# A graph layer on one core: each row transfer of blocks 9 to 117 waits for TensorE at the same share of the next block's work

## The chip, the core and the metric

The kernel runs on one core of one Trainium2 chip. The core has a matrix engine (TensorE, PE in the profile; its weight loads are shown apart as PEld), three engines for elementwise work (VectorE or DVE, ScalarE or ACT, GpSimd or POOL), a sync engine (SP) that starts transfers, and 16 DMA engines that move data between the chip's memory and the core's on-chip buffers. The metric is the device time of one execution in microseconds (us); lower is better.

## The reference

A graph has 6250 nodes and 206,250 edges. Each edge passes a message through a small two-layer network; the messages are averaged at the node at one end of the edge, and the result goes through a second network, a residual connection and a layer norm. `x` holds 64 features for each node, `edge_attr_64` 64 for each edge.

```python
edge_index = jnp.stack([src, dst])
row, col = (edge_index[0], edge_index[1])
msg = jnp.concatenate([src_node_features[col], edge_attr], axis=1)
h = jax.nn.relu(msg @ W1a.T + b1a)
h = h @ W1b.T + b1b
sums = jax.ops.segment_sum(h, row, num_segments=n_nodes)
counts = jax.ops.segment_sum(jnp.ones((h.shape[0],), h.dtype), row, num_segments=n_nodes)
agg = sums / jnp.maximum(counts, 1.0)[:, None]
z = jnp.concatenate([src_node_features, agg], axis=1)
z = jax.nn.relu(z @ W2a.T + b2a)
z = z @ W2b.T + b2b
out = jnp.concatenate([z, src_node_features], axis=1) @ Wr.T + br
...
x = _layernorm(x + out, axis=-1, eps=1e-05)
```

Everything is float32. The time lies in the part up to `sums`: the first layer of the edges, and the sum over the edges of each node.

## The kernel before

The edges are cut into tiles of 128, and the tiles into 124 blocks of 13 (`NG`, `BLK`; `NGR` is 124). For each block the kernel computes the first layer's output `h` of its 1664 edges (128 features plus two columns, so rows of 130 floats), and GpSimd writes these rows out to a table in the chip's memory, each row at a slot that depends on the edge's node, so that the rows of nearby nodes come to lie together (a bin is 128 nodes). Later, groups of the table are read back (`rt`, line 1454) and summed by node: a matmul with a one-hot matrix (line 1502), in small pieces spread over the following blocks.

**How a tile's rows come about.** In blocks 4 to 103 the first tiles of a block are joined in threes: TensorE multiplies one-hot marks by the loaded data (`join`, line 1264, six matmuls 512 wide, whose result ScalarE copies at line 1269), which lays the 384 edges of three tiles into 128 groups of four places, and then computes their messages (`join_rows`, line 1277, finished by ScalarE at line 1280). The output of a join is written by one transfer, called a quad (line 1363). A block has two joins (six tiles), or three in the odd blocks from 9 to 25 (`THRICE`), or none below 4 and from 104 on. The other tiles of a block are direct: line 1352 multiplies, ScalarE applies the relu into `orow` (line 1355), and each tile is written by a transfer of its own (line 1392), called a row transfer. So GpSimd issues 9 transfers for a block with two joins, 7 with three, 13 with none. `orow` is a ring of four blocks (`ROWS`).

**One iteration** of the loop handles block k. On TensorE it holds, in this order: the counts for block k+1 (lines 1091 to 1130), a first part of the direct tiles, a first part of a group of sums (`sum_first`), the last direct tiles, the joins, the rows of the joins, and the rest of the sums (`sum_rest`). Where sums are due faster, more of them follow.

**What sets the order.** The order of TensorE, ScalarE, VectorE and SP is written out by hand. GpSimd's queue is not: a scheduler lays out the transfers by the time at which it expects their inputs, and an instruction waits in the queue behind those ahead of it. `scatter(k)` emits the transfers of block k, and it runs two iterations behind (`LEAD`). In blocks 9 to 117 (`PACED`) some row transfers also wait for a named instruction of TensorE in iteration k+1, taken from the dictionary `done`: the last matmul of a direct tile (`done[k, c]`), of a join's rows (`"join0"` and so on), of the first half of the sums (`"first"`), or of their rest (`"rest"`). With two joins (`j0` is 6) four of the seven row transfers have such a wait; with three joins three of the four, since the block behind has only two joins; with none four of thirteen, since the block behind has no join. The others, and the quads, wait only for their own data and the queue.

## Time and profile before

| | before |
|---|---|
| median of 3 runs | 2108.51 us (2105.86 to 2118.02) |
| the profiled execution, its own time | 2113.43 us |
| span of the profiled execution | 2111.6 us |
| mean granted TensorE clock | 0.874 |
| TensorE busy, matmuls | 1648.5 us, 78% |
| VectorE busy | 1376.4 us, 65% |
| GpSimd busy | 1153.6 us, 55% |
| ScalarE busy | 1105.0 us, 52% |

The page of the profile gives busy times, an overview of the span in 40 slices, the chain of work that ended last, and the costliest groups of instructions, with what ended the idle time ahead of them. A timeline lists single instructions with their start, their duration and the idle time of their engine before them. A table of windows gives, for stretches of the span, the busy time of each engine and in brackets the number of its instructions, then the granted TensorE clock (1.00 is full), the mean busy share of the DMA engines, and GB/s. "Issue" is time in which an engine waited for nothing that the profile shows; "remote" and "another core or an unknown queue" are releases that the profile can't place. There is one core here, so these aren't other cores.

In the profiled execution, blocks 9 to 26 run from about 185 to 360 us, blocks 27 to 103 from there to about 1528, and the blocks without joins from there to about 2050, of which the last six, 118 to 123, are not in `PACED`.

### The profile page before, as it was taken

To read this page: it belongs to the slowest core of one execution; us is meant where nothing else is said; L and a number is where in the kernel's file an instruction comes from. 1 tells how busy PE (TensorE), PEld (TensorE's weight loads), DVE (VectorE), ACT (ScalarE), POOL (GpSimd) and SP (SyncE) were. 2 spreads that over 40 slices of the span, in tenths; PEclk is the share of its full clock that TensorE was granted. 3 is DMA by queue.
4 is the path that set the end of the run, shared out by engine and by line. 5 is a ranking of instruction groups with operands and counts; after the bars stand their busy time and mean duration, and the time that the engine had idled before them with its cause. 6 is when DMAs were issued, how large, how long until landed. Compare 5 with 4: busy or idle time off the path is not lost.

```text
span 2111.6 us, 33441 instructions
## 1 busy us (share of the span) xinstructions
PE 1648.5 (78%) x10901; PEld 1455.0 (69%) x10901; DVE 1376.4 (65%) x3210; ACT 1105.0 (52%) x2246; POOL 1153.6 (55%) x1268
## 2 busy tenths in 40 slices
PE   5577877768887888788778887877867778677787
PEld 4466766657776777677667776776767667566676
DVE  5377777656667777677776777776755555454377
ACT  2257777666666566566666666656622223222007
POOL 6464655565555566566665665655655545544400
PEclk7578988889999899999998999989978878777899
DMA  6556667665656567566556555555668667565472
GB/s 163 162 171 220 234 224 243 214 211 176 209 183 204 169 201 211 169 195 188 181 174 182 175 173 163 186 157 170 168 201 277 200 190 208 170 183 172 147 216 66
DMA packets 243142, 396.32 MB, mean 188 GB/s; under 512 B 43621, under 2 KB 177895, under 8 KB 242703
## 3 DMA queue, kind: packets, MB, share of 16 engines
q1 hardware_dynamic: 162109, 225.24, 37.7%
q0 software_dynamic: 48240, 121.28, 16.4%
q10 hardware_dynamic: 32610, 47.58, 6.5%
q8 instruction: 89, 1.46, 0.3%
q14 instruction: 94, 0.77, 0.1%
HBM read 218.49 MB, written 175.44 MB: 187 GB/s over the span
## 4 chain that ended last, share of the span: by engine, by line
PE 57%; issue 11%; DVE 10%; ACT 10%; another core or an unknown queue 8%; DMA 3%; POOL 1%; SPq 0%; ACTq 0%; DVEq 0%; POOLq 0%
PE h_ps L1502 22%; PE h_ps L1264 10%; PE h_ps L1352 9%; PE h_ps L1277 7%; DVE oh L1483 2%; DVE marks L1232 2%; ACT rhs L1317 2%; ACT rj L1269 1%; ACT orow L1355 1%; DMA rows<-orow,rowidx 1%; DMA rt<-rows 1%; ACT orow L1280 1%; ACT marks L1237 1%; PE cnt_ps L1091 1%
## 5 line engine op out<-in xcount | busy, mean ns | idle before, releaser
L1392 POOL DMA_INDIRECT rows<-orow,rowidx x985 | 947.2, 962 | 769.4 <-issue 207.4
L1502 PE MATMUL h_ps<-rt,oh 128*128 128x129 f32 x4056 | 602.3, 303 | 126.4 <-issue 105.4
L1502 PEld LDWEIGHTS h_ps<-rt,oh 128*128 128x128 f32 x4056 | 554.3, 215 | 151.9 <-issue 135.7
L1355 ACT ACTIVATE orow<-h_ps 128x384 f32<-128x384 f32 (+1 forms) x287 | 153.3, 537 | 657.5 <-PE h_ps L1352 360.7
L1277 PE MATMUL h_ps<-mv,rj 128*128 128x130 f32 x1672 | 256.1, 305 | 136.3 <-ACT rj L1269 73.5
L1264 PE MATMUL h_ps<-marks,side 128*128 128x512 f32 x1254 | 343.7, 423 | 23.8 <-ACT xr_now L1652 10.6
L1277 PEld LDWEIGHTS h_ps<-mv,rj 128*128 128x128 f32 x1672 | 232.6, 210 | 174.4 <-ACT rj L1269 89.1
L1562 DVE TENSOR_TENSOR part<-part,h_ps 128x387 f32<-128x387 f32 (+2 forms) x249 | 122.6, 493 | 312.5 <-remote 147.7
L1483 DVE TENSOR_TENSOR oh<-ramp,rt 128x768 f32<-128x768 bf16 (+3 forms) x440 | 321.3, 765 | 7.2 <-DMA rt<-rows 7.0
L1352 PE MATMUL h_ps<-mv,rhs 124*128 124x128 f32 x1970 | 297.3, 298 | 16.8 <-issue 9.2
L1264 PEld LDWEIGHTS h_ps<-marks,side 128*128 128x128 f32 x1254 | 245.1, 204 | 79.5 <-issue 11.6
L1352 PEld LDWEIGHTS h_ps<-mv,rhs 124*128 124x128 f32 x1970 | 267.1, 209 | 20.4 <-issue 10.6
L1232 DVE TENSOR_TENSOR marks<-quad_ramp,ramp 128x1024 fp32r<-128x1024 f32 x209 | 250.9, 1204 | 0.0
L1363 POOL DMA_INDIRECT quads<-orow,qidx x209 | 200.4, 959 | 88.8 <-ACT orow L1280 39.1
L1280 ACT ACTIVATE orow<-h_ps 128x260 f32<-128x260 f32 x418 | 142.6, 388 | 90.8 <-PE h_ps L1277 28.0
L1105 DVE TENSOR_SCALAR of_quads<-cnt_ps 128x98 bf16<-128x98 f32 x100 | 26.6, 266 | 247.0 <-remote 84.2
L1269 ACT COPY rj<-h_ps 128x512 f32<-128x512 f32 x209 | 118.8, 588 | 120.8 <-PE h_ps L1264 67.6
L1238 ACT ACTIVATE marks<-marks,ones 128x512 fp32r<-128x512 f32 x209 | 151.0, 722 | 6.8
L1237 ACT ACTIVATE marks<-quad_ramp,z_act 128x512 fp32r<-128x512 f32 x209 | 149.5, 715 | 0.0
L1049 DVE TENSOR_TENSOR_SCAN had<-ramp,bins 128x400 bf16<-128x400 bf16 (+1 forms) x124 | 135.0, 1089 | 14.9 <-ACT bins L1070 1.2
L1315 ACT ACTIVATE rhs<-rhs,from_win 60x896 f32<-60x896 bf16 (+1 forms) x116 | 130.4, 1124 | 2.8
L1317 ACT ACTIVATE rhs<-rhs,ones 60x896 f32<-60x896 f32 (+1 forms) x116 | 130.2, 1123 | 2.9
(189 smaller groups left out, 1535.6 us busy)
## 6 DMA issues: line engine op xcount, KB each, us to landing
rt<-rows SPq DMA_DIRECT2D x138, 390.0 KB
rt<-quads SPq DMA_DIRECT2D x98, 390.0 KB
rhs<-in_edgeT SPq DMA_DIRECT2D x91, 224.0 KB
rt<-rows SPq DMA_DIRECT2D x103, 195.0 KB
enat<-in_edgeJ SPq DMA_DIRECT2D x91, 192.0 KB
rows<-orow,rowidx POOLq DMA_INDIRECT x985
rows<-padrow ACTq DMA_DIRECT2D x12, 1300.0 KB
quads<-padrow ACTq DMA_DIRECT2D x11, 1300.0 KB
```

The lines of the kernel that those rows point to most:

```text
L1232: nc.vector.tensor_tensor(m[:, :n, :], all_q[:, None, :].to_broadcast([P, n, QUAD * P]), z[:, :n, None].to_broadcast([P, n, QUAD * P]), op ...
L1237: nc.scalar.activation(m[:, t, :], all_q, AF.Square, bias=z_acts[k][:, i * JOIN + t : i * JOIN + t + 1], scale=-1.0)
L1264: nc.tensor.matmul(ps, s[:, p, i * JOIN + t, :], m[:, t, :], start=t + p == 0, stop=t == JOIN - 1 and p == 1,)
L1277: done[k, f"join{i}"] = nc.tensor.matmul(ps[:, j, :], rj[:, (g0 + j) * P : (g0 + j + 1) * P], m, start=True, stop=True).ins.name
L1280: nc.scalar.activation(mrow[:, g0 : g0 + 2, :], ps, AF.Relu)
L1317: nc.scalar.activation(rhs[D:WIDE, :], rhs[D:WIDE, :], AF.Relu, bias=ones[D:WIDE, :1], scale=-1.0)
L1352: done[k, c] = nc.tensor.matmul(ps[:, j, :], rhs[:WIDE, of * P : (of + 1) * P], m[:WIDE, :H], start=True, stop=True).ins.name
L1355: nc.scalar.activation(orow_of(k, k0, n)[:, :, :H], ps[:, :n, :], AF.Relu)
L1363: s = nc.gpsimd.indirect_dma_start(out=qep.rows.rearrange("(q r) f -> q (r f)", r=QUAD), out_offset=bass.IndirectOffsetOnAxis(ap=qidx[:, q ...
L1392: s = nc.gpsimd.indirect_dma_start(out=ep_.rows, out_offset=bass.IndirectOffsetOnAxis(ap=rowidx[:, k % RING * BLK + j : k % RING * BLK + j ...
L1483: nc.vector.tensor_tensor(res[:, at_tile : at_tile + nb * n, :], ramp[:, None, :].to_broadcast([P, nb * n, P]), node[:, :, None].to_broadc ...
L1502: m = nc.tensor.matmul(of_bin(b), oh[:, at_tile, :], rt[:, j * n + t, : H + 1], start=t0 + t == st.lo[b], stop=t0 + t == st.hi[b] - 1,)
```

## The change

The dictionary `pace` goes, and with it `done`. Every piece of TensorE's work in an iteration now notes its size and its last matmul in `phases`: a group of direct tiles counts 4·H for each tile, a join 2·3·4·128, a pair of a join's rows 8·W, a piece of sums 4·(H+1) for each of its tiles. Every row transfer of blocks 9 to 117 then waits for the last piece of block k+1 whose cumulated work is not above a share of the whole. The share rises evenly with the tile's number, and the quads, which have no such wait, count as the first transfers.

```diff
+        phases = [[] for _ in range(NGR + 1)]
+        def phase(k, work, name):
+            phases[k].append(((phases[k][-1][0] if phases[k] else 0) + work, name))
+        def reached(k, share):
+            names = [name for at, name in phases[k] if at <= share * phases[k][-1][0]]
+            return names[-1] if names else phases[k - 1][-1][1]
...
-            pace = (
-                {9: BLK - 1, 10: "join0", 11: "join1", 12: "join2"} if j0 == 3 * JOIN
-                else {6: 9, 8: BLK - 1, 10: "join0", 12: "join1"} if j0 == 2 * JOIN
-                else {j0: 9, j0 + 2: "first", 7: BLK - 1, 9: "join0", 11: "rest"}
-            )
...
-                later = (min(k + 1, NGR - 1), pace.get(j))
-                if k in PACED and later in done:
+                later = reached(k + 1, (j - j0 + joined(k)) / (BLK - j0 + joined(k))) if k in PACED else None
+                if later:
                     tc.add_manual_dep(
-                        s.ins, done[later],
+                        s.ins, later,
                         mybir.DependencyInfo(mybir.DependencyClass.Sync, mybir.DependencyReason.DATA),
```

The order of TensorE, ScalarE, VectorE and SP is the same in both programs, and so are TensorE's waits. GpSimd's order and waits differ from the first paced blocks on.

The first place is GpSimd's queue around block 41, in the stage with two joins. `orow_141` to `orow_144` are the ring's buffers, here for blocks 40, 41, 42 and 43; `rows_64` is the table of the direct tiles' rows, `quads` that of the joins. `DMASW` is one of the queue's own eight counters, `PE_49`, `DVE_49` and `Activation_49` are waits for TensorE, VectorE and ScalarE. Before, in iteration 41:

```order
L1392 DMA rows_64<-orow_141,rowidx 125440x130 [waits DMASW3_49,PE_49]
L1392 DMA rows_64<-orow_142,rowidx 125440x130 [waits DMASW4_49,DVE_49,Activation_49]
L1392 DMA rows_64<-orow_142,rowidx 125440x130 [waits DMASW5_49]
L1392 DMA rows_64<-orow_141,rowidx 125440x130 [waits DMASW6_49,PE_49]
L1392 DMA rows_64<-orow_142,rowidx 125440x130 [waits DMASW7_49,Activation_49]
L1392 DMA rows_64<-orow_141,rowidx 125440x130 [waits DMASW0_49,PE_49]
L1363 DMA quads<-orow_142,qidx 54976x520 [waits DMASW1_49,DVE_49,Activation_49]
L1392 DMA rows_64<-orow_141,rowidx 125440x130 [waits DMASW2_49,PE_49]
L1363 DMA quads<-orow_142,qidx 54976x520 [waits DMASW3_49,Activation_49]
```

And now, from the first row transfer of block 41, which waits for iteration 42:

```order
L1401 DMA rows_64<-orow_142,rowidx 125440x130 [waits DMASW1_49,PE_49]
L1401 DMA rows_64<-orow_142,rowidx 125440x130 [waits DMASW2_49,PE_49]
L1401 DMA rows_64<-orow_142,rowidx 125440x130 [waits DMASW3_49,PE_49]
L1401 DMA rows_64<-orow_142,rowidx 125440x130 [waits DMASW4_49,PE_49]
L1401 DMA rows_64<-orow_142,rowidx 125440x130 [waits DMASW5_49]
L1401 DMA rows_64<-orow_142,rowidx 125440x130 [waits DMASW6_49,PE_49]
L1401 DMA rows_64<-orow_142,rowidx 125440x130 [waits DMASW7_49,PE_49]
L1377 DMA quads<-orow_143,qidx 54976x520 [waits DMASW0_49,DVE_49,Activation_49]
L1377 DMA quads<-orow_143,qidx 54976x520 [waits DMASW1_49,Activation_49]
```

Before, three rows of the block's own iteration stood between four of the block before it. Now all seven rows of a block stand together, each behind TensorE's work on the next block, and the two quads of that next block follow them. In iteration 42, which has 85 matmuls in the trace, the waits of before fall behind matmuls 13, 39, 59 and 67, and those of now behind 33, 39, 45, 51, 59 and 67, the rows without a wait of their own behind the one ahead of them.

The second place is the same queue in the stage without joins, around block 110, whose rows are in `orow_143` (`orow_142` is block 109). Before, in iteration 110:

```order
L1392 DMA rows_64<-orow_143,rowidx 125440x130 [waits DMASW4_49,DVE_49,Activation_49]
L1392 DMA rows_64<-orow_143,rowidx 125440x130 [waits DMASW5_49]
L1392 DMA rows_64<-orow_142,rowidx 125440x130 [waits DMASW6_49,PE_49]
L1392 DMA rows_64<-orow_143,rowidx 125440x130 [waits DMASW7_49,Activation_49]
L1392 DMA rows_64<-orow_143,rowidx 125440x130 [waits DMASW0_49]
L1392 DMA rows_64<-orow_143,rowidx 125440x130 [waits DMASW1_49]
L1392 DMA rows_64<-orow_142,rowidx 125440x130 [waits DMASW2_49,PE_49]
L1392 DMA rows_64<-orow_143,rowidx 125440x130 [waits DMASW3_49,Activation_49]
L1392 DMA rows_64<-orow_143,rowidx 125440x130 [waits DMASW4_49]
L1392 DMA rows_64<-orow_143,rowidx 125440x130 [waits DMASW5_49,Activation_49]
L1392 DMA rows_64<-orow_143,rowidx 125440x130 [waits DMASW6_49]
L1392 DMA rows_64<-orow_142,rowidx 125440x130 [waits DMASW7_49,PE_49]
```

And now, the rows of block 110 from the first on:

```order
L1401 DMA rows_64<-orow_143,rowidx 125440x130 [waits DVE_49,DMASW0_49,PE_49,Activation_49]
L1401 DMA rows_64<-orow_143,rowidx 125440x130 [waits DMASW1_49,PE_49]
L1401 DMA rows_64<-orow_143,rowidx 125440x130 [waits DMASW2_49,PE_49]
L1401 DMA rows_64<-orow_143,rowidx 125440x130 [waits DMASW3_49,PE_49]
L1401 DMA rows_64<-orow_143,rowidx 125440x130 [waits DMASW4_49,PE_49,Activation_49]
L1401 DMA rows_64<-orow_143,rowidx 125440x130 [waits DMASW5_49,PE_49]
L1401 DMA rows_64<-orow_143,rowidx 125440x130 [waits DMASW6_49]
L1401 DMA rows_64<-orow_143,rowidx 125440x130 [waits DMASW7_49,PE_49,Activation_49]
L1401 DMA rows_64<-orow_143,rowidx 125440x130 [waits DMASW0_49]
L1401 DMA rows_64<-orow_143,rowidx 125440x130 [waits DMASW1_49,PE_49]
L1401 DMA rows_64<-orow_143,rowidx 125440x130 [waits DMASW2_49,Activation_49]
L1401 DMA rows_64<-orow_143,rowidx 125440x130 [waits DMASW3_49,PE_49]
```

Here the change goes the other way: nine of these twelve rows had no wait for TensorE, and now three have none. In iteration 110, which has about 120 matmuls in the trace, the waits of before fall behind matmuls 24, 42, 80 and 120, and those of now behind 12, 18, 24, 36, 42, 56, 68, 80, 92, 106 and 120.

More of the change, by code (lines that the diff above doesn't have):

```diff
@@ L1263, in join @@
                 for p in range(2):
-                    nc.tensor.matmul(
+                    name = nc.tensor.matmul(
                         ps, s[:, p, i * JOIN + t, :], m[:, t, :],
                         start=t + p == 0, stop=t == JOIN - 1 and p == 1,
-                    )
+                    ).ins.name
+            phase(k, 2 * JOIN * QUAD * P, name)
             rj = turned[k, i] = top.rjs[(join_at[k] + i) % 2]
@@ L1276, in join_rows @@
                 for j in range(2):
-                    done[k, f"join{i}"] = nc.tensor.matmul(
+                    name = nc.tensor.matmul(
                         ps[:, j, :], rj[:, (g0 + j) * P : (g0 + j + 1) * P], m, start=True, stop=True
                     ).ins.name
+                phase(k, 4 * W * 2, name)
                 nc.scalar.activation(mrow[:, g0 : g0 + 2, :], ps, AF.Relu)
@@ L1333, in fast_path @@
         made = {}
-        done = {}
+        phases = [[] for _ in range(NGR + 1)]
[4 more added lines that the diff above has]
+            return names[-1] if names else phases[k - 1][-1][1]
         def low_bits(k):
@@ L1351, in hidden @@
                     of = c - (BLK - direct(k))
-                    done[k, c] = nc.tensor.matmul(
+                    name = nc.tensor.matmul(
                         ps[:, j, :], rhs[:WIDE, of * P : (of + 1) * P], m[:WIDE, :H], start=True, stop=True
                     ).ins.name
+                phase(k, 4 * H * n, name)
                 nc.scalar.activation(orow_of(k, k0, n)[:, :, :H], ps[:, :n, :], AF.Relu)
@@ L1492, in summed @@
         def summed(st, reads, oh, of_bin, bins=None):
-            at_tile = 0
+            at_tile, work = 0, 0
             for b0, nb, t0, n, rt in reads:
@@ L1506, in summed @@
                         at_tile += 1
-            return m.ins.name
+                        work += 4 * (H + 1)
+            return work, m.ins.name
         def reads_of(st):
@@ L1570, in sum_first @@
             g.half = range(g.b0, g.b0 + -(-g.nb // 2))
-            done[k, "first"] = summed(g.st, g.reads, g.oh, lambda b: g.ps[:, b - g.b0, :], g.half)
+            phase(k, *summed(g.st, g.reads, g.oh, lambda b: g.ps[:, b - g.b0, :], g.half))
             return g
@@ L1575, in sum_rest @@
             if g.nb > len(g.half):
-                done[k, "rest"] = summed(
+                phase(k, *summed(
                     g.st, g.reads, g.oh, lambda b: g.ps[:, b - g.b0, :], range(g.half.stop, g.b0 + g.nb)
-                )
+                ))
             totals.append(g)
```

1 line of the change is left out of this document (removed).

## The prediction

> **What bounds the kernel now.** I read the chain of waits first, for no engine is busy all the time.
>
> ```profile
> PE 57%; issue 11%; DVE 10%; ACT 10%; another core or an unknown queue 8%; DMA 3%; POOL 1%; SPq 0%; ACTq 0%; DVEq 0%; POOLq 0%
> ```
>
> TensorE's own work is 57% of the chain, and 19% is time for which the profile names no cause; on a span of 2111.6 us that is some 400 us. GpSimd, the engine whose queue the change rewrites, is 1%. So the second look goes to GpSimd's groups, the page's row and then what waits for it:
>
> ```profile
> L1392 POOL DMA_INDIRECT rows<-orow,rowidx x985 | 947.2, 962 | 769.4 <-issue 207.4
> ...
> L1483 DVE TENSOR_TENSOR oh<-ramp,rt 128x768 f32<-128x768 bf16 (+3 forms) x440 | 321.3, 765 | 7.2 <-DMA rt<-rows 7.0
> ```
> ```profile
> L1392 POOLq EVENT_SEMAPHORE  x720: 17/17/14378, 12.5 to 2001.5; - x180
> ...
> who waited for it (us, times):
>   POOL rows L1392: 0.9, 3
> ```
>
> A transfer holds GpSimd for 0.96 us, and no other engine waits for one; the sums, which read the rows back, lost 7 us to that in all. The transfers would seem free. That they aren't shows where they come in long unbroken runs. Here are five windows in the stage without joins; behind the span come TensorE's matmuls (the first bracket), its weight loads, VectorE, ScalarE, GpSimd, the clock.
>
> ```profile
> 1857.30:1863.30 6.00, 6.00 (x53) 5.78 (x52) 5.83 (x12) 2.63 (x4) 4.28 (x5) 0.97 0.91 234
> 1863.30:1869.70 6.40, 4.19 (x29) 3.28 (x27) 1.73 (x3) 2.07 (x3) 4.33 (x5) 1.00 0.53 159
> 1869.70:1875.80 6.10, 3.67 (x12) 2.89 (x13) 2.16 (x3) 1.17 (x3) 4.79 (x5) 0.63 0.36 92
> 1875.80:1881.80 6.00, 2.69 (x8) 1.75 (x7) 0.00 (x0) 0.00 (x0) 2.88 (x3) 0.50 0.21 73
> 1881.80:1887.80 6.00, 6.00 (x40) 6.00 (x41) 5.04 (x8) 0.00 (x0) 0.00 (x0) 0.74 0.81 271
> ```
> ```profile
> 1857.29 0.96 POOL L1392 DMA_INDIRECT rows<-orow,rowidx  x1 [7.07 <-PE h_ps L1502]
> 1858.55 0.95 POOL L1392 DMA_INDIRECT rows<-orow,rowidx  x1 [0.30 <-PE cnt_ps L1092]
> ...
> 1868.48 0.96 POOL L1392 DMA_INDIRECT rows<-orow,rowidx  x1 [0.90 <-remote]
> ...
> 1878.58 0.96 POOL L1392 DMA_INDIRECT rows<-orow,rowidx  x1 [0.30 <-issue]
> 1888.65 0.95 POOL L1392 DMA_INDIRECT rows<-orow,rowidx  x1 [9.11 <-PE h_ps L1502]
> ```
>
> A run of seventeen transfers starts at 1857.3, one each 1.26 us (1858.55 − 1857.29), with no pause longer than the 0.90 us at 1868.48. For its first 6 us TensorE does 53 matmuls, 8.8 each us; then the rate falls, to 12 in 6.1 us (2.0 each us), and it stays there until the run ends at 1878.6. Two to three microseconds later TensorE is back. The run isn't a result of TensorE's slowness, for GpSimd hardly waits in it. The same at another place, with six transfers in the first window and seven in the second:
>
> ```profile
> 1649.00:1655.50 6.50, 6.50 (x61) 6.50 (x60) 4.64 (x10) 4.86 (x6) 4.12 (x6) 1.00 0.95 278
> 1655.50:1663.90 8.40, 3.74 (x23) 3.31 (x21) 1.16 (x2) 1.01 (x3) 6.55 (x7) 0.75 0.50 140
> ```
>
> So a run may be some five transfers long; what goes beyond that costs TensorE. I call this starving; why it happens the profile doesn't show, only that the 19% without a cause are partly this. Where the runs are short, nothing of the kind is seen. This is GpSimd in the stage with two joins, block 41:
>
> ```profile
> 633.01 0.96 POOL L1392 DMA_INDIRECT rows<-orow,rowidx  x1 [1.16 <-PE cnt_ps L1095]
> 634.27 0.96 POOL L1363 DMA_INDIRECT quads<-orow,qidx  x1 [0.30 <-ACT bins L1070]
> ...
> 638.06 0.96 POOL L1392 DMA_INDIRECT rows<-orow,rowidx  x1 [0.30 <-issue]
> 640.64 0.96 POOL L1392 DMA_INDIRECT rows<-orow,rowidx  x1 [1.62 <-remote]
> 641.90 0.96 POOL L1392 DMA_INDIRECT rows<-orow,rowidx  x1 [0.30 <-issue]
> 647.29 0.96 POOL L1392 DMA_INDIRECT rows<-orow,rowidx  x1 [4.43 <-PE h_ps L1277]
> ```
>
> The named waits break the nine transfers of an iteration into groups, with pauses between starts of 2.6 us (640.64 − 638.06) and 5.4 us. The stages, and an iteration without any disturbance (two rows of the chain that each begin one):
>
> ```profile
> 185.00:360.00 175.00, 138.43 (x872) 118.12 (x871) 124.43 (x333) 135.70 (x279) 103.17 (x107) 0.88 0.70 234
> 360.00:1528.00 1168.00, 953.72 (x6487) 837.75 (x6487) 832.59 (x2015) 750.50 (x1485) 694.97 (x724) 0.92 0.60 185
> 1528.00:1845.00 317.00, 233.66 (x1577) 217.98 (x1575) 160.98 (x271) 81.56 (x113) 169.41 (x178) 0.81 0.68 207
> ```
> ```profile
> 928.54 0.17 PE cnt_ps L1091
> ...
> 939.92 0.17 PE cnt_ps L1091
> ```
>
> In the stage with two joins 724 transfers at nine a block are 80 iterations of 14.5 us (1168/80.4); undisturbed, one takes 11.4 us (939.92 − 928.54). So 3.1 us of each are lost to something, part of it already starving. The stage without joins has 178 transfers, thirteen a block: 13.7 iterations of 23.1 us.
>
> **The change, part by part.** *Two joins (77 blocks, 27 to 103).* Nine transfers, as before, but the three rows that went ahead in the block's own iteration are held, and all seven rows follow each other behind marks that lie 6 to 8 matmuls apart (33 to 67 of 85). At 8.8 matmuls a microsecond a mark is passed each 0.7 to 0.9 us, faster than GpSimd's 1.26. So once the first is passed the others don't hold the queue back, and the two quads behind them, which need the joins, are ready as the rows end. The nine become one run: eight steps of 1.26 are 10.1 us. TensorE is good for the first 6.0, starved until about 2.4 us after the last start (between 1878.58 and 1881.8), so for 6.5 us at 2.0 instead of 8.8 matmuls: 6.5 · (1 − 2.0/8.8) = 5.0 us lost. On 11.4 that is 16.4, against 14.5 now: +1.9 us, 77 times, **+146**. The bounds: if TensorE, once slow, reaches the last marks late, so that two of the nine fall off the run, seven are left; starved from 6.0 to 7.6 + 2.4, 4.0 · 0.77 = 3.1 us, the iteration is 14.5 and the cost nothing. If only half of the 3.1 us lost now is starving and the rest stays, 11.4 + 1.5 + 5.0 = 17.9, +3.4 each and +262. I take +146, which lies between the two. Behind a held row wait the quads, and behind them nothing but later rows; who waits for those was shown above: nobody.
>
> *Three joins (18 blocks, 9 to 26, of which nine have three).* Seven or nine transfers, the runs in part broken by the shorter blocks. Half of the price above, 18 · 0.95 = +17, between 0 and 18 · 1.9 = +34.
>
> *No joins (14 blocks, 104 to 117).* Here most rows had no wait and ran eleven and more in a row; now they have marks 6 to 14 matmuls apart. Marks at 0.7 to 1.6 us (6 to 14 at 8.8) are no slower than GpSimd's own 1.26 as long as TensorE is quick, so that a run still forms; but once TensorE falls to 2.0 a microsecond a mark takes 3 to 7 us, the run breaks, and TensorE recovers. Without any starving 115 matmuls (1577/13.7) would take 13.1 us at 8.8, and GpSimd's thirteen take 16.4, so at most 23.1 − 16.4 = 6.7 us of an iteration are to be had. A loss I exclude, since it would need runs longer than those that are there now. I take a third of the 6.7, because the first five or six marks still pass quickly and the low clock stays: 14 · 2.2 = **−31**, between 0 and 14 · 6.7 = −94.
>
> *The clock.* A spell of 6.5 us may be answered by a lower granted clock: in the windows above it is 0.63 and 0.50 in the spell, and the 6 us behind it have 40 matmuls at 0.74 where 53 were done at 0.97, so 13/8.8 = 1.5 us lost for a spell of 12 us and more. In the second place, of 8.4 us, the clock was still 0.75. I charge 1.5 us on a quarter of the 77 spells, +29; the bounds are 0 and 77 · 1.5 = +116. [...]
>
> *The waits themselves.* Some 300 more waits of GpSimd for TensorE, fewer for ScalarE: they lie in the queue's 0.30 us between two transfers, I charge 0; at the 17 ns that the median event takes on GpSimd's queue (in the row above) it would be 5 us.
>
> The sum: 146 + 17 − 31 + 29 = +161 on the profiled execution's own 2113.4 (a span of 2111.6 and 1.8 around it), 2274; it stands 5 us above the median of the runs, so **2270**.
>
> **The rivals.** *The transfers are hidden anyway.* Nobody waits for them, in the rows above; TensorE's slowness would come from what it reads, and only fall together with the runs. Then the time stays, 2108 ± 10. Against it speaks that the rate falls at the same age of a run at both places and returns as it ends. [...] The windows above, 12 matmuls in 6.1 us with GpSimd's transfers beside them, don't look like it, but they don't show the cause either.
>
> *Only the stage without joins counts (faster).* With two joins the runs break at the marks, for TensorE when starved gets to them late, as in the lower bound above: 0 there, and without joins two thirds of its bound, −63, with 0 for the rest: 2108 − 63, about 2045. It decides from the point at which runs with two joins stay at seven or below. Against it: the seven rows and two quads lie behind marks that are already passed when GpSimd comes to them.
>
> *Each spell takes the clock down (much slower).* With 1.5 us on all 77 instead of a quarter, 87 more, and a third of the way to the first term's upper bound, 39 more: 161 + 87 + 39 on 2108, about 2395. For it, the 0.50 above; against it, 0.75 in a spell of 8.4 us.
>
> *The runs break at eight (little slower).* One transfer waits for a mark, eight are left: starved from 6.0 to 8.8 + 2.4, 5.2 us, of which 4.0 are lost; 15.4 an iteration, +0.9 · 77 = +69, with −31 and +17 about 2160. It stands between the forecast and the first term's lower bound, and what speaks for it is the same lateness of the marks.
>
> **How the numbers follow.** The forecast, starving at about 2270 (2200 to 2330), 0.47; broken at eight, 0.17; the clock, 0.16; hidden anyway, 0.08; faster, 0.12. About 0.5%, 10.5 us, is what a measurement of this kernel tells from no change. Slower by more: 0.47 + 0.17 + 0.16 = 0.80; within: 0.08; faster: 0.12. The range leaves out the faster case and the far end of the clock's: 2100 to 2385; the forecast's own is 2200 to 2330.
>
> **What would show it.** In the changed kernel's profile GpSimd's timeline at blocks 27 to 103 should show eight or nine starts 1.26 us apart and then a pause of 4 us or more; the window of that stage should last 1300 us or more with the same number of matmuls; issue and the unknown queue should rise above 19% of the chain; the stage without joins should be the same or shorter. I am wrong if the two-join runs are long and TensorE keeps its rate in them (then starving is no effect of runs), or if they come in groups of five and fewer (then the marks do pace).

## The result, and the profile after

| | before | after |
|---|---|---|
| median | 2108.5 us (2105.86 to 2118.02, 4 runs) | 2192.49 us (2176.72 to 2196.46, 4 runs) |
| ratio to before | | 1.037 (95% interval 1.033 to 1.042) |
| span of the profiled execution | 2111.6 us | 2188.4 us |
| mean granted TensorE clock | 0.874 | 0.870 |

The change makes the kernel 3.7% slower, 84 us where 161 were forecast. The chain of waits of the changed kernel, to be held against that of before, where PE had 57%:

```profile
PE 40%; DVE 18%; another core or an unknown queue 14%; issue 13%; ACT 8%; DMA 3%; POOL 3%; ACTq 0%; DVEq 0%; SPq 0%; POOLq 0%
```

Time without a named cause rose from 19% to 27%. TensorE's own work is the same. The windows tell where it happened. They are cut at the starts of blocks 9, 27, 104, 118 and 123, which one copy of ScalarE in each block marks (line 1343 before, 1356 after); the columns are those of the prediction. Before, then after:

```profile
176.10:415.50 239.40, 191.63 (x1170) 163.07 (x1169) 169.32 (x461) 180.35 (x367) 134.53 (x141) 0.87 0.68 229
415.50:1528.40 1112.90, 909.81 (x6230) 800.85 (x6229) 795.08 (x1908) 713.28 (x1412) 664.98 (x694) 0.93 0.60 184
1528.40:1845.00 316.60, 233.26 (x1574) 217.69 (x1571) 160.94 (x270) 81.19 (x112) 169.32 (x177) 0.81 0.68 207
1845.00:1973.70 128.70, 94.99 (x604) 86.20 (x605) 61.25 (x97) 25.15 (x37) 61.82 (x66) 0.75 0.57 174
```
```profile
173.70:431.60 257.90, 193.77 (x1179) 164.46 (x1178) 171.25 (x463) 180.24 (x367) 131.40 (x137) 0.88 0.62 211
431.60:1646.80 1215.20, 952.74 (x6224) 845.82 (x6223) 793.21 (x1909) 718.47 (x1412) 667.56 (x691) 0.89 0.55 168
1646.80:1919.90 273.10, 216.84 (x1575) 203.01 (x1574) 162.97 (x271) 79.96 (x113) 164.90 (x173) 0.88 0.79 240
1919.90:2050.00 130.10, 94.84 (x612) 85.47 (x610) 59.78 (x95) 24.88 (x36) 70.96 (x75) 0.79 0.56 175
```

With equal counts of work, blocks 9 to 26, half of which have three joins, take 18.5 us more, blocks 27 to 103 with two joins 102.3 more (1.33 an iteration), blocks 104 to 117 without joins 43.5 less; the last blocks, which the change leaves alone, 1.4 more. Block 27 of before starts at 415.5 us and not at about 360, as was said above: some of the 724 transfers that the prediction counted in its window are those of earlier blocks, but its 14.5 us for an iteration stands (1112.9 in 77). GpSimd in the two-join stage of after, and the windows around one of its runs:

```profile
1095.75 0.96 POOL L1401 DMA_INDIRECT rows<-orow,rowidx  x1 [1.67 <-remote]
1099.84 1.09 POOL L1401 DMA_INDIRECT rows<-orow,rowidx  x1 [3.13 <-PE h_ps L1511]
1101.23 0.96 POOL L1401 DMA_INDIRECT rows<-orow,rowidx  x1 [0.30 <-issue]
...
1107.55 0.96 POOL L1377 DMA_INDIRECT quads<-orow,qidx  x1 [0.30 <-issue]
1108.81 0.96 POOL L1377 DMA_INDIRECT quads<-orow,qidx  x1 [0.30 <-issue]
1115.25 0.96 POOL L1401 DMA_INDIRECT rows<-orow,rowidx  x1 [5.48 <-PE h_ps L1511]
```
```profile
1099.80:1107.10 7.30, 6.54 (x45) 5.67 (x45) 5.36 (x15) 3.71 (x8) 5.74 (x6) 1.00 0.34 98
1107.10:1111.10 4.00, 0.86 (x8) 0.69 (x7) 0.00 (x0) 2.03 (x5) 2.06 (x3) 1.00 0.61 128
1111.10:1115.25 4.15, 3.53 (x23) 3.36 (x23) 3.74 (x8) 3.47 (x6) 0.00 (x0) 0.72 0.78 285
```

Six rows and two quads start within 9 us. For 7.3 us TensorE does 45 matmuls; in the next four it does 8, until 2.3 us after the last start (1111.1 − 1108.81). From the end of the last quad on, GpSimd stands still for 5.5 us, since its next row waits for a mark that TensorE has not reached. Both halves of what the prediction argued are here. Its count is not: counting the transfers of blocks 27 to 103 whose starts lie less than 1.6 us apart as one run, the profile of after has 21 runs of eight, 19 of seven and 15 of six, and none of nine (three, if the limit is 1.7 us); before it had 14 of seven, 20 of six and two longer ones. Transfers beyond the fifth of a run rose from 55 to 116.

The breaks lie at the marks. Of the 77 iterations of after, the first row starts 1.6 us or more behind the transfer ahead of it in 65, the second in 38, the seventh in 28, each of the others in at most 12, and the quads once in 154. Beyond the usual 1.26 us these pauses are 199 us ahead of the first row, 74 ahead of the second and 30 ahead of the seventh.

Where TensorE stops in this run the timeline tells, and the waits of the whole stage, before and then after, show that it is no single case (us in total, times, longest):

```profile
1111.38 0.26 DVE L1105 TENSOR_SCALAR of_quads<-cnt_ps 128x98 bf16<-128x98 f32 x1 [6.04 <-remote]
1111.69 0.29 PE L1118 MATMUL cnt_ps<-joh,before_w 128*128 128x300 bf16 x1 [3.73 <-DVE of_quads L1105]
```
```profile
PE cnt_ps L1118 <- DVE of_quads L1105: 46.8, 33, 4.8
DVE of_quads L1105 <- remote: 48.2, 10, 7.6
```
```profile
PE cnt_ps L1118 <- DVE of_quads L1105: 146.3, 47, 6.3
DVE of_quads L1105 <- remote: 245.7, 46, 10.3
```

The profile puts TensorE's stop of 3.7 us down to VectorE. The counts at the start of an iteration go from TensorE to VectorE, which makes `of_quads` of them (line 1105), and back (line 1118). VectorE starts `of_quads` only after 6.0 us of idle time, at 1111.38, and what released it the profile can't place. All of TensorE's idle time ahead of line 1118 rose from 56.8 to 180.3 us in the stage, while that ahead of the joins' rows (line 1277 before, 1278 after) fell from 112.7 to 66.2. So the stage's loss shows mostly at this round trip; which of the two engines ran short first in it the profiles of the layer don't show.

### The profile page after: what moved, and what is told of

Same layout as the page of the kernel before. It is cut to its first block, busy times and chain, and to the rows that moved or that the text cites. A ratio compares the mean times of both kernels' runs of the same rounds, so it can differ in the third digit from the quotient of the medians.

```text
span 2188.4 us, 33778 instructions
## 1 busy us (share of the span) xinstructions
PE 1672.0 (76%) x10901; PEld 1483.2 (68%) x10901; DVE 1375.3 (63%) x3210; ACT 1108.2 (51%) x2246; POOL 1158.6 (53%) x1268
## 4 chain that ended last, share of the span: by engine, by line
PE 40%; DVE 18%; another core or an unknown queue 14%; issue 13%; ACT 8%; DMA 3%; POOL 3%; ACTq 0%; DVEq 0%; SPq 0%; POOLq 0%
PE h_ps L1511 19%; PE h_ps L1365 7%; PE h_ps L1264 5%; PE h_ps L1278 4%; DVE marks L1232 4%; DVE oh L1492 3%; POOL rows L1401 2%; DVE part L1572 1%; DMA quads<-orow,qidx 1%; ACT rj L1270 1%; ACT orow L1369 1%; DVE hit_q L1160 1%; ACT rhs L1319 1%; DMA rt<-rows 1%
## 5 line engine op out<-in xcount | busy, mean ns | idle before, releaser
L1511 PE MATMUL h_ps<-rt,oh 128*128 128x129 f32 x4056 | 611.1, 308 | 91.0 <-issue 70.3
L1511 PEld LDWEIGHTS h_ps<-rt,oh 128*128 128x128 f32 x4056 | 566.3, 220 | 110.6 <-issue 102.1
L1365 PE MATMUL h_ps<-mv,rhs 124*128 124x128 f32 x1970 | 318.4, 311 | 30.1 <-issue 18.8
L1492 DVE TENSOR_TENSOR oh<-ramp,rt 128x768 f32<-128x768 bf16 (+3 forms) x440 | 321.1, 764 | 11.8 <-DMA rt<-rows 11.8
L1365 PEld LDWEIGHTS h_ps<-mv,rhs 124*128 124x128 f32 x1970 | 287.6, 222 | 39.4 <-issue 26.2
L1278 PE MATMUL h_ps<-mv,rj 128*128 128x130 f32 x1672 | 237.7, 289 | 85.2 <-ACT orow L1282 28.3
L1278 PEld LDWEIGHTS h_ps<-mv,rj 128*128 128x128 f32 x1672 | 216.1, 195 | 118.7 <-ACT orow L1282 36.0
L1118 PE MATMUL cnt_ps<-joh,before_w 128*128 128x300 bf16 x100 | 34.4, 344 | 246.8 <-DVE of_quads L1105 188.8
L1120 PEld LDWEIGHTS <-one_w 128*128 128x128 bf16 x200 | 21.6, 108 | 267.5 <-issue 261.4
```

The source lines that it names most:

```text
L1278: name = nc.tensor.matmul(ps[:, j, :], rj[:, (g0 + j) * P : (g0 + j + 1) * P], m, start=True, stop=True).ins.name
L1365: name = nc.tensor.matmul(ps[:, j, :], rhs[:WIDE, of * P : (of + 1) * P], m[:WIDE, :H], start=True, stop=True).ins.name
L1492: nc.vector.tensor_tensor(res[:, at_tile : at_tile + nb * n, :], ramp[:, None, :].to_broadcast([P, nb * n, P]), node[:, :, None].to_broadc ...
L1511: m = nc.tensor.matmul(of_bin(b), oh[:, at_tile, :], rt[:, j * n + t, : H + 1], start=t0 + t == st.lo[b], stop=t0 + t == st.hi[b] - 1,)
```

## The experiments

Kernels of one table row ran on one chip with the kernel before beside them, and chips differ: before took 2109, 2083, 2081 and 2082 us on four chips and 1610 us on a fifth, so kernels are compared by the ratio to before on their own chip. "The stage" is blocks 27 to 103.

### One stage at a time, and the last blocks

The waits by share are kept in some blocks, and the named waits of before in the others:

```diff
-PACED = range(PRE, 118)
+PACED = range(PRE, 118)             # late_all: range(PRE, 122)
+BY_SHARE = range(104, 118)          # early_only: range(PRE, 104), late_all: range(104, 122)
...
+                if k in BY_SHARE:
+                    later = reached(k + 1, (j - j0 + joined(k)) / (BLK - j0 + joined(k)))
+                else:
+                    later = done.get((min(k + 1, NGR - 1), pace.get(j))) if k in PACED else None
```

> The waits by share are used in blocks 104 to 117 alone, the named waits of before stay in blocks 9 to 103. Starving theory: in the profiles that stage went from 316.6 us to 273.1 us with the change, because transfers beyond the fifth of an unbroken run fell from 75 to 18; alone it should bring the same, 2108 - 43 = 2065 us (2050 to 2080). Rival, that the added waits themselves cost time wherever they are: no gain, 2108 or more.

> The waits by share are used in blocks 9 to 103 alone, the named waits of before stay from 104 on. If the stages add up, the loss of the two stages with joins, 18 us and 102 us in the profiles, stands by itself: 2108 + 120 = 2228 us (2205 to 2245). If the loss there were made up or caused by what the later stage does, it would be nearer to the 2192 of the change.

> Waits by share in blocks 104 to 121, the last six blocks' four that had no waits included; the named waits of before in blocks 9 to 103. Starving theory: blocks 118 to 121 took 26 us each with runs of up to 13, and go to the 19 to 20 us of the blocks ahead of them, 4 times 6 = 24 us under the 2071 of the waits by share in 104 to 117 alone: 2047 us (2035 to 2062). Rival, that the tail is bound by its loads or the end of the transfers: no difference to 2071.

| | median | before beside it | ratio |
|---|---|---|---|
| late_only | 2070.92 us | 2109.05 us | 0.981 (0.975 to 0.988) |
| early_only | 2220.28 us | 2109.05 us | 1.052 (1.045 to 1.059) |
| late_all | 2029.13 us | 2082.71 us | 0.974 (0.969 to 0.979) |

The stages stand by themselves: 1.052 and 0.981 add up to 1.033, the change had 1.037. Late, the waits by share are a gain in either company, and they are one in blocks 118 to 121 too, which had no waits: blocks 118 to 122 took 95.3 us in the profile of late_all against 128.7 before (the whole times alone, 0.974 and 0.981, don't tell late_all from late_only; its 2029 us lie below the 2035 to 2062 that were expected, on a chip on which before was quicker too). That added waits cost by themselves wherever they are is out.

### The change with pauses between the transfers

In blocks 27 to 103 GpSimd does twelve small memsets behind the second and sixth row; then four.

```diff
+                if held and k in PAUSED:
+                    tc.add_manual_dep(s.ins, held.pop(), ...
...
+                if k in PAUSED and ((j - j0) in (1, 5)):
+                    with tc.issue_after(s.ins):
+                        for _ in range(12):          # pause_short: 4
+                            held[:] = [nc.gpsimd.memset(idle, 0.0).ins.name]
```

> The change, and in blocks 27 to 103 GpSimd also does twelve small memsets (some 1.2 us) behind the second and the sixth row transfer of each block, so that it has more to do, and no run is longer than five. Starving theory: the run's length is what costs; blocks 27 to 103, 1215 us with the change, fall to 1060 to 1130 us and the whole to 2040 to 2105 us. Rival, that the late transfers or their waits cost the time: the pauses make the transfers later still, and the whole stays at 2190 us or rises.

> As the run with pauses, which came out at GpSimd's own time (two pauses of 3.3 us between starts and seven steps of 1.26 are 15.4 us, and the iterations took 15.4), but four small memsets instead of twelve, so that a pause is some 2.1 us from start to start and GpSimd's own time 13.0 us. If the runs' length is what the change lost by, the stage of blocks 27 to 103 goes from 1215 us to 1120 to 1160, and the whole to 1.00 to 1.015 times before. If the loss is that the queue is held once in each iteration, by whatever transfers, the stage stays at 1200 us or rises, 1.03 to 1.06.

> The change with the short pauses again. On a chip of 2100 us: if the runs' length is what the change lost by, 1.00 to 1.015 times before; if the held queue, 1.03 to 1.06. On a chip of 1610 us again 1.08, since the pauses add to GpSimd's own time, which sets the iteration there.

The twelve memsets missed what was expected: 2189.53 us, 1.039 (1.031 to 1.046), where 2040 to 2105 were expected. Its GpSimd timeline points to the reason:

```profile
907.69 0.95 POOL L1404 DMA_INDIRECT rows<-orow,rowidx  x1 [0.30 <-PE h_ps L1280]
908.64 0.13 POOL L1425 MEMSET idle<- 128x8 f32 x1
908.95 0.97 POOL L1380 DMA_INDIRECT quads<-orow,qidx  x1 [0.18 <-ACT marks L1239]
909.91 1.74 POOL L1425 MEMSET idle<- 128x8 f32 x11
912.26 0.96 POOL L1404 DMA_INDIRECT rows<-orow,rowidx  x1 [0.61 <-issue]
```
```profile
ACT orow L1359 <- DMA rows<-orow,rowidx: 251.8, 42, 12.8
```

A pause took 3.3 us from start to start (912.26 − 908.95) and not 2.2, so that GpSimd alone needs 15.4 us for a block, and that is what an iteration took (1187.1 us in 77). The transfers had become the bound, and ScalarE waited 252 us for them to leave the ring `orow`, a wait that none of the lists of before or after has among its longer ones. So this kernel tells little of runs and starving. The short pauses, beside the change on one chip (after_again), in the stage, the change first:

```profile
437.70:1635.90 1198.20, 946.21 (x6222) 839.11 (x6221) 793.23 (x1908) 717.72 (x1411) 665.35 (x691) 0.89 0.56 171
```
```profile
418.50:1562.40 1143.90, 918.50 (x6236) 817.13 (x6234) 793.00 (x1909) 714.55 (x1411) 731.83 (x1296) 0.91 0.58 179
```

The change was at 1.031 (1.023 to 1.038) of before there, with the pauses at 1.010 (1.006 to 1.014), as expected of the runs' length. GpSimd has 605 instructions more to do and the stage is 54 us shorter; transfers beyond the fifth of a run fell from 125 to 34. Two thirds of the loss went, without a wait taken away. This is the experiment that ties the loss to the runs; the third that stayed it doesn't explain.

### No waits, and earlier waits

no_wait takes the named waits of before out of blocks 27 to 103 (the change isn't in it); even and half count the share of the change from 0 and from half as many quads.

```diff
-PACED = range(PRE, 118)
+PACED = (*range(PRE, 27), *range(104, 118))          # no_wait
...
-                later = reached(k + 1, (j - j0 + joined(k)) / (BLK - j0 + joined(k))) if k in PACED else None
+                later = reached(k + 1, (j - j0) / (BLK - j0 + joined(k))) if k in PACED else None                  # even
+                later = reached(k + 1, (j - j0 + joined(k) / 2) / (BLK - j0 + joined(k))) if k in PACED else None  # half
```

> The kernel before without the named waits in blocks 27 to 103: no row transfer of these waits for TensorE's work on the next block; the waits elsewhere are those of before. Starving theory (a run of transfers beyond five or six starves TensorE): runs get longer, the 77 iterations go from 14.5 to 15.5 to 16.5 us, the whole to 2185 to 2260 us. Rival, the held queue (an iteration is GpSimd's nine transfers, 11.4 us, and the time that its queue is held at marks): nothing is held, the iterations fall towards 12 to 13 us, the whole to 1920 to 2000 us.

> The change with the share counted from zero: with two joins the seven rows wait for 0 to 6 ninths of the next block's work instead of 2 to 8 ninths. Starving theory: marks still pass faster than GpSimd issues, runs are as long as with the change, 2190 us within 25. Held queue: the queue isn't held for the first third of an iteration any more, the 77 iterations of 15.8 us fall to 13 to 14.5 and the whole to 1980 to 2090 us.

> The change with the share counted from half as many quads (with two joins from 1 to 7 ninths): between the change (2 to 8 ninths, 1.037 times before) and the share from zero (0 to 6 ninths, 0.978). If the place of the run in TensorE's work decides, the time lies between, 0.99 to 1.02. If only the first wait of all matters, at zero, it is that of the change, 1.03 to 1.04.

> The change with the share counted from half as many quads. On a chip of 2100 us between the change (1.03 to 1.037 times before) and the share from zero (0.978): 0.99 to 1.02, if it is how the run lies in TensorE's work that decides; 1.03 or more if only a first wait at zero helps. On a chip of 1610 us 1.0025 again.

| | median | before beside it | ratio | the stage, profiled | beyond the fifth |
|---|---|---|---|---|---|
| before | 2108.5 us | | 1 | 1112.9 us | 55 |
| after | 2192.49 us | 2108.5 us | 1.037 | 1215.2 us | 116 |
| no_wait | 2202.76 us | 2082.71 us | 1.063 (1.055 to 1.071) | 1224.8 us | 169 |
| even | 2035.02 us | 2082.71 us | 0.978 (0.972 to 0.983) | 1086.7 us | 47 |
| half_again | 2084.09 us | 2082.1 us | 1.001 (0.998 to 1.004) | 1146.3 us | 97 |

no_wait settles the sign of the waits of before in this stage: with no transfer held at a mark the stage takes 1224.8 us instead of 1112.9, where the rival, that an iteration is made of the time that the queue is held, expected it to get faster. The named waits earned their place. With the change itself no_wait can be compared in the stage alone, for the change also gains 43.5 us in the late blocks: 1224.8 and 1215.2 us, about the same.

even went against the starving theory as I had put it, which expected runs as long as with the change and 2190 us; its 2035 us lie in the range that the held queue gave, 1980 to 2090. The runs came out shorter than before, and the time with them. Waits that begin two ninths of an iteration's work earlier fall differently into TensorE's work: in its profile pauses of 1.6 us or more lie ahead of the third row of a block in 27 of the 77 iterations, ahead of the fourth in 33 and ahead of 32 of the quads, in the middle of what would be a run, and the pauses ahead of the first row are 52 us in all instead of 199. Half lies between. Why earlier marks break the runs I had not foreseen and did not test apart, so that in even the shorter runs and the shorter holding of the queue can't be told from each other. The held queue alone is out by no_wait.

Over the chips of the table the stage follows the transfers beyond the fifth: 47, 55, 97, 116, 169 go with 1087, 1113, 1146, 1215, 1225 us. It isn't one price, though: the step from 55 to 169 (no_wait) is 1.0 us for each of them, that from 55 to 116 (after) 1.7. And outside the table the order breaks: the short pauses have 34 and 1144 us, more than before with 55, and the best version below has 54 and 1080. The count is a sign of starving, not a measure of it.

### What starves

Two small kernels compute nothing of the layer. TensorE, VectorE and ScalarE each repeat one instruction that waits for no other engine, while GpSimd issues row transfers in runs.

```diff
+            for i in range(PE_N):
+                nc.tensor.matmul(ps[i % 4], w, m, start=True, stop=True)
+            for i in range(DVE_N):
+                nc.vector.tensor_add(a2, a, a)
+            for i in range(ACT_N):
+                nc.scalar.copy(b2, b)
```

> Not the layer: none of it is computed, the output is zeros. TensorE, VectorE and ScalarE each repeat one instruction that waits for no other engine; GpSimd issues row transfers of 128 rows of 130 floats in unbroken runs of 3, 4, 5, 6, 7, 8, 9 and 13, each followed by a long pause, then groups of four with short pauses of four lengths, then the runs again while the sync engine also loads. Starving theory: TensorE's weight loads keep their rate in runs up to five and fall to a quarter some 6 to 7 us after a longer run began, until about 2.4 us after its last start. If TensorE's slowness came from its data dependencies, or from loads, its rate is flat here, at least in the first part.

> The first small kernel again, nothing of the layer. On a chip of 2100 us TensorE falls from nine weight loads each microsecond to one or two some 7 us into a run, as in the first run. On a chip of 1610 us: if it is the supply of instructions that GpSimd's transfers cut off on the other chips, it isn't cut off here, and TensorE keeps nine loads each microsecond through runs of thirteen and more.

> Not the layer: none of it is computed, the output is zeros. As the first small kernel, but TensorE's matmuls are 512 wide (about four times fewer weight loads each microsecond), VectorE repeats a tiny instruction (one element a partition, near ten each microsecond), ScalarE as before; GpSimd's runs are 4 to 9, 13 and 20 transfers. If a run starves whoever takes many instructions, VectorE now slows some 6 to 8 us into a run and TensorE later or not at all. If it starves TensorE alone (its reads, its port), TensorE falls again at 7 us and VectorE keeps its rate.

In the first, around a run of thirteen that begins at 345.2 us, its first 7 us and then ten more:

```profile
345.20:352.20 7.00, 7.00 (x65) 7.00 (x65) 6.62 (x12) 6.65 (x12) 5.45 (x6) 1.00 0.16 51
353.20:363.20 10.00, 2.59 (x9) 1.74 (x8) 9.44 (x17) 9.49 (x17) 7.29 (x28) 0.71 0.16 54
```

65 matmuls in 7 us, then 9 in 10, with nothing to wait for and the DMA engines 16% busy. VectorE and ScalarE, with 17 instructions each in those 10 us, keep their rate. In runs of five hardly anything is seen (33 weight loads in the 4 us from 22.7, where a run of five ends); in the run of seven that starts at 39.4 us, 5 weight loads are left in the two microseconds from 47.4. So TensorE's slowness is no matter of its data, and a run causes it. The second kernel gives TensorE wide matmuls and VectorE a tiny operation; a run of twenty starts at 86.5 us:

```profile
86.50:89.50 3.00, 3.00 (x8) 1.33 (x7) 2.77 (x44) 2.87 (x5) 2.39 (x3) 1.00 0.16 48
89.50:114.50 25.00, 24.78 (x58) 10.83 (x57) 4.55 (x38) 23.75 (x40) 17.72 (x39) 1.00 0.15 48
114.50:118.00 3.50, 3.34 (x8) 1.51 (x8) 3.37 (x56) 3.34 (x6) 2.67 (x79) 1.00 0.02 5
```

Now VectorE falls from 15 a microsecond (44 in 3 us) to 1.5 (38 in 25), after 3 us already, and TensorE, with 2.3 matmuls and as many weight loads each microsecond, isn't touched up to the end of the run (busy for 24.78 of the 25 us). So in these two kernels it is neither one engine nor its data: the engine with the most instructions starves, TensorE with 9.3 matmuls and as many weight loads each microsecond in the first, VectorE with 15 in the second. What was left to it was 1.7 a microsecond for TensorE in the first kernel (9 matmuls and 8 weight loads in 10 us) and 1.5 for VectorE in the second. That isn't a fixed share for each engine, since TensorE kept 4.6 in the second (115 in 25 us). The first kernel ran again on another chip, 786.73 us against 786.63, and starves there alike: 65 matmuls in the first 7 us of its run of thirteen, then 9 in 10.

Two more things stand in these traces. VectorE with its tiny operation starves in short runs too, here in one of five that starts at 9.1 us, 31 instructions in its first 2 us and 18 in the next 5:

```profile
9.10:11.10 2.00, 2.00 (x6) 0.82 (x5) 1.82 (x31) 0.00 (x0) 1.68 (x2) 1.00 0.37 93
11.10:16.10 5.00, 5.00 (x13) 2.28 (x12) 1.65 (x18) 0.00 (x0) 3.83 (x23) 1.00 0.47 120
```

And short pauses were not enough for TensorE at nine weight loads each microsecond. The first kernel also issues groups of four, first with pauses of 1.6 us from start to start, one of 2.8 among them, and then with pauses of 2.2 us. TensorE is left with 85 weight loads in 28.6 us and 166 in 30.6:

```profile
189.40:218.00 28.60, 17.56 (x86) 14.13 (x85) 26.97 (x48) 27.20 (x44) 22.08 (x81) 0.69 0.14 47
229.30:259.90 30.60, 24.76 (x166) 21.51 (x166) 28.83 (x52) 29.10 (x48) 23.71 (x121) 0.94 0.14 45
```

That it is the supply of instructions, as I supposed ahead of micro_again, and what in a transfer stops it, no run here shows, nor why TensorE goes on for 7 us of a run (65 matmuls) and VectorE for 3 (44 instructions). TensorE's matmuls were not slowed in the second kernel: the 58 in the 25 us of the run took 427 ns each (24.78/58), those of the whole kernel 431 (431.1/1000). But the rival that the transfers are hidden is out: in the first kernel TensorE, with nothing to wait for, did 9 matmuls in 10 us of a run.

### The best version

The named waits of before in blocks 9 to 26, the share from zero in 27 to 121, that is `PACED = range(PRE, 122)`, `BY_SHARE = range(27, 122)` and the share of even.

> The named waits of before in blocks 9 to 26, the share from zero in blocks 27 to 121. If the stages add up: 0.974 times before (the waits by share to block 121) and 26 us less in blocks 27 to 103 (1113 to 1087 us with the share from zero), 0.962 (0.95 to 0.972). If the stages work against each other, no better than 0.974.

> Named waits in blocks 9 to 26, the share from zero in 27 to 121. On a chip of 2100 us 0.95 to 0.972 times before if the stages add up; on a chip of 1610 us 1.008 again, since there is no starving to avoid.

> The changed kernel once more, beside the others of this call. On a chip where the kernel before takes 2100 us: 1.033 to 1.042 times it, as measured. On a chip where it takes 1610 us and runs of a hundred transfers leave TensorE its rate: if starving carries the loss, the change is within 1% of before there (0.995 to 1.01); if the held queue costs time by itself, 1.03 or more there too.

> The changed kernel a third time, in case the chip is one of those on which long runs leave TensorE its rate (before 1610 us): there 0.995 to 1.01 times before if starving carries the loss, 1.03 or more if the held queue costs time by itself. On a chip of 2100 us: 1.025 to 1.042 again.

| | median | before beside it | ratio |
|---|---|---|---|
| best, on the fifth chip | 1621.21 us | 1609.88 us | 1.008 (1.006 to 1.009) |
| half, on the fifth chip | 1614.38 us | 1609.88 us | 1.003 (1.001 to 1.004) |
| pause_short, on the fifth chip | 1739.21 us | 1609.88 us | 1.080 (1.078 to 1.082) |
| best_again | 2005.22 us | 2080.75 us | 0.964 (0.958 to 0.971) |
| after_again | 2148.87 us | 2080.75 us | 1.031 (1.023 to 1.038) |
| after_third | 2150.48 us | 2082.1 us | 1.035 (1.028 to 1.042) |

On a chip of the usual kind the stages add up and best is 3.6% faster than before. On the fifth chip half has in its profile, in the stage:

```profile
321.90:1201.60 879.70, 818.93 (x6224) 741.11 (x6223) 790.37 (x1912) 714.16 (x1412) 659.82 (x685) 1.00 0.77 232
```
```profile
699.55 0.95 POOL L1401 DMA_INDIRECT rows<-orow,rowidx  x1 [0.60 <-PE h_ps L1365]
700.80 0.95 POOL L1401 DMA_INDIRECT rows<-orow,rowidx  x1 [0.30 <-issue]
702.06 0.96 POOL L1401 DMA_INDIRECT rows<-orow,rowidx  x1 [0.30 <-PE h_ps L1365]
```

The same 6224 matmuls in 880 us, with GpSimd in runs that include one of 463 transfers (from 667 to 1254 us, starts less than 1.7 us apart), and TensorE at 7 weight loads each microsecond. An iteration is 11.4 us, nine transfers of 1.26. Nothing of the starving is seen on this chip, GpSimd's queue is the bound, and breaking runs with pauses gained nothing: pause_short took 129 us more than before (1.080), nearly what its pauses last, for two in a block of 2.17 us from start to start instead of 1.26 (918.75 − 916.58 in the profile of pause_short_again) are, as an estimate, 140 us in 77 blocks. What differs on this chip no run shows. The change itself did not run on it, so what it does there stays open; half and best suggest within 1%.

## What the prediction had right, and which step failed

**The direction and the cause that was named: borne out.** The change is slower, it loses in the two-join stage, and runs of transfers do starve TensorE, also where TensorE waits for nothing (9 matmuls in 10 us of the bare kernel's run of thirteen, after 65 in 7). The sums, which read the rows back, waited 11.8 us for it in all where they had waited 7, so little was lost there, as said.

**Two joins, +146: the step that failed.** The stage measured +102.3 in the two profiles. The step is "So once the first is passed the others don't hold the queue back [...] The nine become one run". The marks do hold it: ahead of the second row in 38 of the 77 iterations, 74 us in all, and ahead of the seventh in 28, so that runs end at eight and fewer. The lower bound of the term had this ("TensorE, once slow, reaches the last marks late"), though it is more often the second mark than the last ones. The price of a run failed as well. The onset was put too early: 6.0 us, from a run in the stage without joins; in the run shown above TensorE goes on for 7.3 us, and for 7 to 8 in the bare kernel (65 matmuls in the first 7 us of a run, 9 in the ten from 8 us on). With a run of eight and an onset of 7.3 the working's own arithmetic gives (8.8 + 2.4 − 7.3) · 0.77 = 3.0 us lost in an iteration instead of 5.0, and 11.4 + 3.0 is 14.4, no loss against before. But an iteration of after takes 15.8 us (1215.2 in 77). So the corrected sum misses the whole of the 1.33 us, and that the forecast came as near as it did is in part luck: a rate of TensorE alone, by the age of a run, doesn't price this stage. What it left out is that the engines wait for each other: TensorE's idle time at the round trip to VectorE rose by 123.5 us, 1.6 an iteration, and fell by 46.5 ahead of the joins' rows. How the 102.3 us divide into starving, that round trip and the hold ahead of the first rows stays open.

**The clock, +29: not a term of its own.** The two-join stage's clock fell from 0.93 to 0.89, and whatever that cost lies within its 102 us; the whole kernel's went from 0.874 to 0.870, since the stage without joins gained (0.81 to 0.88). With the clock's 29 that stage was forecast at +175.

**Three joins, +17:** measured +18.5. **No joins, −31:** measured −43.5, within its bounds of 0 to −94; the third that was credited was nearer to a half; late_only, which has it alone, took 265.7 us there. **The waits themselves, 0:** not measured apart.

Together: 102.3 + 18.5 − 43.5, with −2.4 and +1.9 at the two ends that the change leaves alone, are the 76.8 us between the spans, where 161 were forecast. Of the 84 too many, 44 are the two-join runs, 29 the clock, 12 the stage without joins. The rival "the runs break at eight" (2160) described the runs best, and the time came out between it and the forecast; its own price for a run, 4.0 us from the onset of 6.0, has the same fault. Of the other rivals, "hidden anyway" falls with the bare kernel, "only the stage without joins counts" with early_only, and "each spell takes the clock down" (2395) with the time and a clock of 0.870.

## What to carry to other kernels

Indirect transfers that nobody waits for can still set the time: short pauses between those of the change took the stage from 1198.2 to 1143.9 us, without a wait taken away. Look at the rate of the engine with the most instructions by the age of a run of back-to-back transfers, and break such runs. How short a run and how long a pause must be depends, by these runs, on that engine: pauses of some 2.2 us gave the layer two thirds of its loss back (1.031 to 1.010), but left TensorE 5.4 of its nine weight loads each microsecond in the first bare kernel (166 in 30.6 us), and a run of five starved VectorE in the second (31 instructions in 2 us, then 18 in 5). When a wait is hung on an engine that the run itself slows, count the feedback: the wait breaks the run that was priced, here ahead of its second row in 38 of 77 iterations. Before pricing a slow engine by its own rate, look for the round trips to other engines on which its idle time falls, here 180.3 us instead of 56.8 ahead of line 1118. And an effect of this kind is to be measured on more than one chip, since one of five did not have it.

## What the runs showed of the hardware

In long runs of indirect transfers the engine with the most instructions got few in both bare kernels: of TensorE's 9.3 matmuls each microsecond, each with its weight load, 0.9 were left in the first (9 in 10 us, at a DMA share of 0.16), of VectorE's 15 instructions 1.5 in the second (38 in 25 us). Engines that asked for less kept their rate: ScalarE with 1.7 (17 in those 10 us, 12 in the run's first 7), and in a run of 25 us TensorE with 2.3 matmuls and their weight loads (58 and 57). In a run of twenty VectorE kept its rate for the first 3 us (44 instructions), in one of five for the first 2 (31, then 18 in 5 us); TensorE kept its own for the first 7 us of a run of thirteen (65 matmuls). In the layer TensorE was back 2.3 us after the last start of a run (1111.1 − 1108.81). Groups of four with pauses of 2.2 us from start to start still left TensorE only 166 weight loads in 30.6 us. On one chip of five nothing of it was seen (6223 weight loads in 879.7 us of half's stage, 7 each microsecond, with a run of 463 transfers in it), and before took 1610 us there instead of 2080 to 2110.
